# The end of the second attention on other engines: probabilities and a norm turned by DMAs, output products moved, sums of w2 in place

## The chip, the cores and the metric

One core of a Trainium2 chip runs the whole program; the others are not used. The metric is the device time of one execution in microseconds. Engines are named as the profile names them: PE (TensorE's products), PEld (its weight loads), DVE (VectorE), ACT (ScalarE), POOL (GpSimd), SP (SyncE, which issues the DMAs).

## The reference

Two transformer layers on x of shape (4, 256, 256) in float32: batches of 256 rows, width 256. Each sublayer takes a layer norm of x and adds its result to x.

```python
x = x + _L0_attn_ref(_layernorm(x), q_kernel, kv_kernel, out_kernel, q_norm_scale, k_norm_scale)
x = x + _L0_ffn_ref(_layernorm(x), w_gate, w_up, w_down)
x = x + _L1_attn_ref(_layernorm(x), W_K, W_Q, W_V, W_O)
x = x + _L1_ffn_ref(_layernorm(x), W1, W2, W3)
```

The first attention has 16 heads of 128 over 8 key and value heads, an RMS norm and a rotation on queries and keys, and a window of 128. The first feed-forward keeps two of each four hidden units. The second attention is causal with 16 heads of 128:

```python
scores = einsum('biph,biqh->biqp', k, q)
masked = scores * mask - 1e10 * (1.0 - mask)
attn = softmax(masked / sqrt(256))
z = einsum('biqp,biph->biqh', attn, v)
out = einsum('df,bqf->bqd', W_O, z_flat)
```

The second feed-forward is silu(x W1) * (x W3), a normalized Walsh-Hadamard transform over its 1024 units, and a product with W2.

## The kernel before

Everything is in float32 on chip. Rows are tiles of 128 partitions (`xs`, eight of them, two for each batch); x stays in SBUF from start to end.

Both attentions run in sixteen units. In the second, unit n is head group g = n // 4 (four heads) of batch b = n % 4. `pipelined` runs stages with lags: at step s it emits `project` of unit s, `score` of unit s - 1 and `attend` of unit s - 2, and behind them whatever `behind[s]` lists. A scheduler then orders the instructions of each engine by what it expects to be ready, within the order of emission and the hints of `issue_after`; each engine works through its own queue in order.

- `project1` makes queries, keys and values of a unit with seven block products instead of eight. `load_group1` and `right_of` prepare weights and their sums (`w_qk`, `t_qk`).
- `probabilities` (L201) takes the scores of two heads from PE, adds the mask and takes row maxima on DVE (L216), makes the bias `nb` (L221), the exponentials on ACT (L226), the reciprocal `rs` of their sums on DVE (L231), and the normalization on POOL (L234). It is called twice for each unit, for heads 0 and 1 and for heads 2 and 3.
- The products with the values need the probabilities turned. For units 0 to 13, `planes` (L253) has POOL split the float32 words of two heads into their two 16-bit halves (`pl`, L251), SP issues one DMA that transposes them (`plT`, L260), and `joined` (L263) puts the halves together again, the first head on ACT and the second on DVE (L271). For units 14 and 15, `transposed` (L239) turns them on PE (`tr_p`, L246) into PSUM and copies them out on ACT and DVE (L247).
- `attend` makes the values' products (`av`, L279 and L282) and copies them to `zT1` on ACT (L730).
- `project_out1` (L287) is the output product of one unit: sixteen records on PE (`po`, L291) and two additions into x on DVE (L297). Units 0 to 8 have theirs in steps 3 to 11, unit 12 in step 15; those of 9, 10, 11, 13, 14 and 15 stand in step 17.

`normed` (L160) makes a layer norm of one batch and turns it, either on PE (`tr_n`, L182) or, with `by_dma`, by two splits on POOL, a DMA transpose (`xplT`, L192) and two copies on ACT (L195). The second feed-forward begins with the norm of batch 0, which stands in step 16.

The second feed-forward's weights are prepared while the second attention runs. `hadamard` transforms w2: four products on PE (`ph`, L815), copied by ACT into a buffer `a`, then sums and differences on POOL in three rounds from `a` to `b`, back to `a`, and to `b` (L828); `a` and `b` are new tiles under the tags `qkw` and `qkt`. `factors_ffn1` (L839) makes the sums of w1 and w3 for one half of the hidden units, eight subtractions `t_gu` on DVE (L644), under the tag `qkw` for half 0 and `qkt` for half 1. Both halves are prepared in step 16. The tags have two buffers each, shared with the weights `w_qk` and `t_qk` of the head groups.

In the first attention, `project0` (L434) makes queries (weights `wq`) and keys and values (`wkv`) for the two row tiles of a unit. The order is queries of tile 0, keys and values of tile 0, queries of tile 1, keys and values of tile 1. Behind each product DVE makes the two parts of the rotation (`qs`, `qc`, L454), ACT the squares (L459), and for keys and values the copy of v. `rotate0` adds the parts (L473), reduces the squares (`ss`, L474), and has POOL raise the sums to a power (`r`, L493) and scale the keys (L496), which PE then turns (`tr_k`, L522).

Of the kernel before, what the change touches and what calls it, by code (L numbers as in the profile page):

```python
# [20 lines left out]
F32 = mybir.dt.float32  # L21
BF16 = mybir.dt.bfloat16
U16 = mybir.dt.uint16
AF = mybir.ActivationFunctionType
ALU = mybir.AluOpType
AX = mybir.AxisListType

P = 128
B, T, D = 4, 256, 256
NT = T // P  # L30
NC = D // P
HD = 128
NH = 16
FF = 1024
NF = FF // P
# [13 lines left out]
def two_layers(ctx, tc, consts, tables, x, wq, wkv, wo, w_gate, w_up, w_down,  # L49
               w_k, w_q, w_v, w_o, w1, w3, w2, out):  # L50
    nc = tc.nc
# [18 lines left out]
    def half(shape, name):  # L70
        return ps2.tile([P, *shape], F32, tag="half", name=name)
# [7 lines left out]
    def page(name):  # L79

        return work.tile([P, 4, T], F32, tag="page", name=name, bufs=8)
# [28 lines left out]
    tab = page("tables").rearrange("p f t -> p (f t)")[:, 0:768]  # L110
# [3 lines left out]
    wq_sb, wkv_sb = attn_weight("wq"), attn_weight("wkv")  # L114
# [29 lines left out]
    last_of = {}  # L144
# [108 lines left out]
    def planes(p, tile):  # L253


        s = tile([P, 2, 2 * 3 * P], "pl")
        words = p.rearrange("p j n -> p (j n)").bitcast(U16)
        copy_gpsimd(s, words.rearrange("p (n w) -> p w n", w=2))
        sT = tile([P, 12, P], "plT")
        nc.sync.dma_start_transpose(sT, s.rearrange("p w n -> p (w n)"))  # L260
        return sT
# [63 lines left out]
    def attention0():  # L325
        with tc.tile_pool(name="attn0", bufs=2, reuse_waits="tile", side="right") as own:
# [12 lines left out]

            def project(n, _):  # L340
                b, g = divmod(n, 4)
                held = project0(own, xnT[b], g, cos_s, sin_s)
                if g == 1 and b + 1 < B:
                    factors[b + 1] = moments(b + 1)
                if g == 2 and b + 1 < B:
                    with tc.issue_after(last_of["qc"].ins):
                        xnT[b + 1] = normed(b + 1, factors[b + 1])
                return held if n < 14 else rotated(n, held)
# [82 lines left out]
                behind, (0, 5, 4, 3, 1, 2, 6),  # L431
            )

    def project0(own, xnT, g, cos_s, sin_s):  # L434


        v = own.tile([P, NT, 2, HD], F32, tag="v", name="v", bufs=5)
        rot = []
        for t in range(NT):
            cols = slice(t * P, (t + 1) * P)  # L440
            sq = own.tile([P, 6, HD], F32, tag="sq", name="sq", bufs=2)
            qc = own.tile([P, 6, HD], F32, tag="qc", name="qc", bufs=4)
            qs = own.tile([P, 6, HD], F32, tag="qs", name="qs")

            for w, hs in ((wq_sb, slice(0, 4)), (wkv_sb, slice(4, 6))):
                pj = half([4, HD], "pj")
                n = hs.stop - hs.start
                for c in range(NC):
                    last_of[0] = nc.tensor.matmul(  # L449
                        pj, lhsT=xnT[:, c, cols], rhs=w[:, g, c, :],  # L450
                        start=(c == 0), stop=(c == NC - 1),
                    )
                for rot_to, tab in ((qs, sin_s), (qc, cos_s)):
                    last_of["qc"] = nc.vector.tensor_tensor(  # L454
                        rot_to[:, hs], pj[:, 0:n],
                        tab[:, t, hs.start // 4, :].unsqueeze(1).to_broadcast([P, n, HD]),
                        ALU.mult,
                    )
                nc.scalar.activation(sq[:, hs], pj[:, 0:n], AF.Square)  # L459
                if n == 2:  # L460
                    last_of["v", t] = nc.scalar.copy(v[:, t, :, :], pj[:, 2:4])
            rot.append((qc, qs, sq))
        return rot, v

    def rotate0(rot, by_dma, first):
# [229 lines left out]
    def attention1(finish_ffn0):  # L695
        left = left1

        def project(n, _):
            g, b = divmod(n, 4)
            if b == 1 and 1 <= g < 3:  # L700
                load_group1(g + 1)
            held = project1(left[b], gw[g])
            if g == 0 and b + 1 < B:
                with tc.issue_after(last_of["sum"].ins):
                    left[b + 1] = left_of(xn1[b + 1])
            if g == 0 and b + 2 < B:
                xn1[b + 2] = normed(b + 2, by_dma=True)
            return held

        def score(n, held):  # L710
            qk, v = held
            ps = [
                probabilities(qk[:, 0], qk[:, 1], (2 * kk, 2 * kk + 1), mask1) for kk in range(2)
            ]
            return ps if n >= B * 4 - 2 else [
                planes(p, page_of_planes) for p in ps
            ], v

        def attend(n, held):
            ps, v = held  # L720
            zT = page("zT1")
            for kk in range(2):
                pT = transposed(ps[kk]) if n >= B * 4 - 2 else joined(ps[kk], (
                    (nc.scalar.copy, slice(0, 1), last_of["copy"]),
                    (nc.vector.tensor_copy, slice(1, 2), last_of["sum"]),
                ))
                av = bank([2, T], "av1")
                for j in range(2):
                    values(v[:, 0, 2 * kk + j, :], v[:, 1, 2 * kk + j, :], pT[:, j], av[:, j, :])
                nc.scalar.copy(zT[:, 2 * kk : 2 * kk + 2, :], av)  # L730
            return zT

        def out(n, kept=False):
            g, b = divmod(n, 4)

            def emit(done):
                if not kept:
                    project_out1(bank([NT, D], "po1"), done[n], gw[g][2], b)
                else:
                    with tc.issue_after(last_of[1].ins):  # L740
                        project_out1(st([P, NT, D], "po1"), done[n], gw[g][2], b)
            return emit

        behind = {n + 3: [out(n)] for n in range(9)}
        behind[0] = [lambda _: finish_ffn0()]

        def prepare(_):
            w2h.extend(hadamard(w2_raw))
            w2h[1](_)

        behind.setdefault(11, []).append(prepare)
        for i in range(12):
            behind.setdefault(11 + i // 4, []).append(
                lambda _, i=i: w2h[2][i](last_of["planes"].ins)
            )

        def prepare_ffn1(_):
            with tc.issue_after(last_of["sum"].ins):
                r_ffn1.extend(factors_ffn1(half) for half in range(2))

        behind.setdefault(15, []).append(out(12))
        behind[16] = behind.get(16, []) + [
            lambda _: xn_f.append(normed(0)),
            prepare_ffn1,
        ]
        behind[17] = [
            out(9, True), out(13), out(10, True), out(11, True), out(14), out(15),
        ]
        pipelined((project, score, attend), (0, 1, 2), behind, (0, 1, 2))

    def st(shape, name):
# [35 lines left out]
    def hadamard(w2_raw):  # L807


        a, b = (late.tile([P, NF, D], F32, tag=t, name=f"w2_{t}") for t in ("qkw", "qkt"))  # L810

        def within(_):
            for f in range(0, NF, 2):
                ph = bank([2, D], "ph")
                nc.tensor.matmul(  # L815
                    ph, lhsT=had, rhs=w2_raw[:, f : f + 2, :], start=True, stop=True
                )
                nc.scalar.copy(a[:, f : f + 2, :], ph)

        def across(s, src, dst):  # L820
            i = src.rearrange("p (a two s) d -> p a two (s d)", two=2, s=s)
            o = dst.rearrange("p (a two s) d -> p a two (s d)", two=2, s=s)
            half = s * D // 2

            def part(k, op, cols):
                def emit(first):
                    with tc.issue_after(first):
                        nc.gpsimd.tensor_tensor(  # L828
                            o[:, :, k, cols], i[:, :, 0, cols], i[:, :, 1, cols], op
                        )  # L830
                return emit

            return [
                part(k, op, slice(n * half, (n + 1) * half))
                for k, op in enumerate((ALU.add, ALU.subtract)) for n in range(2)
            ]

        return b, within, across(1, a, b) + across(2, b, a) + across(4, a, b)

    def factors_ffn1(half):  # L840

        t = late.tile([P, 2, 4, 2, P], F32, tag=("qkw", "qkt")[half], name="t_gu")
        r = []
        for i, w in enumerate((w1_sb, w3_sb)):
            w = w[:, :, 4 * half : 4 * half + 4, :].rearrange("p c (a m) f -> p c a m f", m=2)
            r.append(right_of(*(w[:, c, :, m, :] for c in range(2) for m in range(2)),
                              [t[:, i, k] for k in range(4)]))
        return r
# [147 lines left out]
```

## Time and profile before

| what | value |
|---|---|
| median of 3 runs | 744.69 us |
| the runs | 744.12, 744.69, 949.75 us |
| the profiled execution | 745.73 us |
| its span, first to last instruction | 743.8 us |
| granted TensorE clock, mean | 1.000 |
| PE busy | 731.7 us |
| DVE, ACT, POOL busy | 464.8, 405.6, 335.1 us |
| first `sc` of unit 15 in the span | 628.80 us |
| first `gu_y` of the second feed-forward | 661.49 us |

Busy time counts when an instruction of the engine was under way. A matmul's end is modelled and its weight load overlaps it, so a busy PE may still hold short waits; the chain of work that ended last shows these as longer pieces. Most float32 products are two records. The times in the text are positions in the span of the profiled execution.

### The profile page before, as it was taken

The numbers are of one execution on the slowest core, as the hardware profiler recorded it, in microseconds if no ns is written. First come the engines' busy times: TensorE is split into PE (matmuls) and PEld (weight loads), VectorE is DVE, ScalarE is ACT, GpSimd is POOL, SyncE is SP. The second block draws the span as 40 slices with busy tenths as digits, with TensorE's granted clock in tenths as the row PEclk, the third lists the DMA queues.
The fourth block names the chain that finished last, engine by engine and source line by source line (L and its number), as shares of the span: only waits on it lengthen the run. The fifth ranks groups of instructions, "written<-read, shape, count | busy, mean of one in ns | idle before, by whom it ended". The sixth has DMA issues, their size and how long they took to land.

```text
span 743.8 us, 11642 instructions
## 1 busy us (share of the span) xinstructions
PE 731.7 (98%) x3952; PEld 598.6 (80%) x3952; DVE 464.8 (62%) x1398; ACT 405.6 (55%) x986; POOL 335.1 (45%) x481
## 2 busy tenths in 40 slices
PE   8999999999999999999999999999999999999998
PEld 5556566566666678888898999999998999899997
DVE  6999877888886516987655644464443548344433
ACT  2487887677768942222356555555555775414432
POOL 1587978887899601011125433343335674221000
PEclk9999999999999999999999999999999999999999
DMA  8733255434453442001324423442232222000100
GB/s 328 286 64 59 49 99 87 77 66 89 82 99 72 85 164 78 15 14 36 108 71 85 129 43 43 88 112 44 44 72 43 44 44 43 1 1 22 22 15 30
DMA packets 127883, 54.88 MB, mean 74 GB/s; under 512 B 121040, under 2 KB 123216, under 8 KB 127056
## 3 DMA queue, kind: packets, MB, share of 16 engines
q1 hardware_dynamic: 127824, 54.15, 31.4%
q8 instruction: 31, 0.51, 0.3%
q14 instruction: 28, 0.23, 0.1%
HBM read 22.94 MB, written 1.05 MB: 32 GB/s over the span
## 4 chain that ended last, share of the span: by engine, by line
PE 85%; DVE 8%; ACT 4%; issue 1%; DMA 1%; POOL 1%; SPq 0%; ACTq 0%; DVEq 0%; POOLq 0%
PE pj L449 10%; PE po L291 7%; PE pgu L554 7%; PE qk_x L781 7%; PE po_f L599 7%; PE po L303 7%; PE sc L214 6%; PE gu_x L856 4%; PE av L279 4%; PE qk_y L781 3%; PE v_x L787 3%; PE av L397 3%; PE sc L213 3%; PE v_zy L787 3%; PE gu_y L856 2%; PE av L282 2%
## 5 line engine op out<-in xcount | busy, mean ns | idle before, releaser
L234 POOL TENSOR_SCALAR p<-p,rs 128x128 f32<-128x128 f32 (+1 forms) x256 | 115.1, 467 | 153.3 <-DVE rs L231 150.0
L251 POOL TENSOR_SCALAR pl<-p 128x1536 uint16<-128x1536 uint16 x58 | 85.3, 1472 | 4.4 <-POOL p L234 0.5
L216 DVE CUSTOM_DVE_ANT_0 p<-sc,cst 128x128 f32<-128x128 f32 (+1 forms) x256 | 79.9, 352 | 11.1 <-PE sc L214 8.6
L271 ACT COPY pT<-plT 128x1536 uint16<-128x1536 uint16 (+1 forms) x58 | 84.0, 1511 | 0.0
L226 ACT ACTIVATE p<-p,nb,r 128x128 f32<-128x128 f32 (+1 forms) x128 | 68.3, 536 | 20.1 <-DVE nb L223 20.1
L449 PE MATMUL pj<-wq,xnT 128*128 128x512 f32 x128 | 61.2, 596 | 1.3 <-DVE qT L512 1.1
L449 PE MATMUL pj<-wkv,xnT 128*128 128x512 f32 x128 | 60.4, 593 | 0.8 <-DMA wkv<-in_wkv_dram 0.8
L226 ACT ACTIVATE p<-p,nb 128x128 f32<-128x128 f32 (+1 forms) x128 | 56.3, 448 | 5.7 <-DVE nb L221 5.7
L303 PE MATMUL po<-wo,zT 128*128 128x256 f32 x256 | 57.8, 379 | 0.0
L291 PE MATMUL po<-w_o,zT 128*128 128x256 f32 x256 | 57.7, 379 | 0.0
L156 POOL TENSOR_SCALAR ve<-mv 128x2 f32<-128x2 f32 (+1 forms) x17 | 4.3, 253 | 115.8 <-DVE mv L152 115.4
L459 ACT ACTIVATE sq<-pj 128x512 f32<-128x512 f32 x64 | 30.9, 490 | 44.0 <-DVE qc L454 43.6
L303 PEld LDWEIGHTS po<-wo,zT 128*128 128x128 f32 x256 | 48.3, 190 | 7.0 <-ACT kT L523 0.6
L291 PEld LDWEIGHTS po<-w_o,zT 128*128 128x128 f32 x256 | 47.5, 190 | 5.8
L449 PEld LDWEIGHTS pj<-wkv,xnT 128*128 128x128 f32 x128 | 24.2, 190 | 31.4 <-issue 28.2
L454 DVE TENSOR_TENSOR qs<-pj,sin_s 128x512 f32<-128x512 f32 x64 | 35.3, 552 | 12.9 <-PE pj L449 12.4
L449 PEld LDWEIGHTS pj<-wq,xnT 128*128 128x128 f32 x128 | 23.5, 190 | 24.4 <-issue 19.6
L670 ACT COPY qk<-qk_x 128x512 f32<-128x512 f32 x16 | 9.4, 586 | 57.6 <-PE qk_x L781 53.0
L279 PE MATMUL av<-pT,v 128*128 128x256 f32 x128 | 38.8, 385 | 0.9 <-ACT pT L271 0.7
L214 PE MATMUL sc<-kT,qT 128*128 128x256 f32 x128 | 38.3, 381 | 0.0
L214 PE MATMUL sc<-qk 128*128 128x256 f32 x128 | 38.2, 380 | 0.0
L251 POOL TENSOR_SCALAR qpl<-qc 128x1024 uint16<-128x1024 uint16 x20 | 28.8, 1451 | 19.1 <-PE av L401 8.3
(155 smaller groups left out, 1757.6 us busy)
## 6 DMA issues: line engine op xcount, KB each, us to landing
w<-in_w_dram SPq DMA_DIRECT2D x3, 1024.0 KB, 4.7
wq<-in_wq_dram SPq DMA_DIRECT2D x4, 512.0 KB, 7.6
wkv<-in_wkv_dram SPq DMA_DIRECT2D x4, 512.0 KB, 8.3
wo<-in_wo_dram SPq DMA_DIRECT2D x4, 512.0 KB, 10.2
w_qk<-in_w_q_dram SPq DMA_DIRECT2D x4, 512.0 KB, 4.5
w_qk<-in_w_k_dram SPq DMA_DIRECT2D x4, 512.0 KB, 5.5
w_v<-in_w_v_dram SPq DMA_DIRECT2D x4, 512.0 KB, 6.5
w_o<-in_w_o_dram SPq DMA_DIRECT2D x4, 512.0 KB, 6.5
```

Of the source, the lines that this page charges most:

```text
L214: nc.tensor.matmul(sc[:, P : 3 * P], lhsT=q[:, P:T], rhs=k, start=True, stop=True)
L216: last_of["mx"] = nc.vector.tensor_tensor_reduce(out=p[:, j, cols], in0=sc[:, cols], in1=mask[:, cols], scale=1.0, scalar=-3.0e38, op0=ALU ...
L226: last_of["exp"] = nc.scalar.activation(p[:, j, cols], p[:, j, cols], AF.Exp, bias=nb[:, j, i : i + 1], scale=SCALE1 if rq is None else rq ...
L234: nc.gpsimd.tensor_scalar(p[:, j, cols], p[:, j, cols], rs[:, j, i : i + 1], 1.0, ALU.mult, ALU.mult)
L251: last_of["planes"] = nc.gpsimd.tensor_scalar(o, i, 1.0, 1.0, ALU.mult, ALU.mult)
L271: copy(words.rearrange("p (n w) -> p w n", w=2), halves[:, :, js].rearrange("p w j n -> p w (j n)"),)
L279: nc.tensor.matmul(av, lhsT=v0, rhs=pT[:, 0:T], start=True, stop=False, skip_group_check=True)
L291: nc.tensor.matmul(po[:, t, :], lhsT=zT[:, j, t * P : (t + 1) * P], rhs=w[:, j, :], start=(t == j == 0), stop=(j == 3), skip_group_check=True,
L303: nc.tensor.matmul(po, lhsT=zTs[hd // 4][:, hd % 4, t * P : (t + 1) * P], rhs=w[:, hd, :], start=(hd == 0), stop=(hd == n - 1),)
L449: last_of[0] = nc.tensor.matmul(pj, lhsT=xnT[:, c, cols], rhs=w[:, g, c, :], start=(c == 0), stop=(c == NC - 1),)
L554: nc.tensor.matmul(o[:, j, :], lhsT=w[:, c, f0 + j, :], rhs=xnT[:, c, :], start=(c == 0), stop=(c == NC - 1),)
L781: last_of[1] = nc.tensor.matmul(o[:, j, :], lhsT=wqk[i - 1][:, j // 2, j % 2, :], rhs=x[i - 1], start=(first and j == 0), stop=True, skip_ ...
```

## The change

Five edits:

- Units 14 and 15 of the second attention go the way of the other units: `planes`, a DMA transpose and `joined`.
- The output products of units 9 and 10 are emitted ahead of the values of unit 14, those of 11 and 13 ahead of the values of unit 15. Those of 14 and 15 stay in step 17.
- The norm of batch 0 for the second feed-forward is turned by DMA.
- `hadamard` uses the tile in which w2 was loaded as its buffer `a`, and `qkw` for `b`. Both halves of `t_gu` are now under the tag `qkt`; half 0 is prepared in step 12, half 1 in step 16.
- In the first unit of the first attention the queries of both tiles come ahead of the keys and values of both.

```diff
@@ project (first attention)
-                held = project0(own, xnT[b], g, cos_s, sin_s)
+                held = project0(own, xnT[b], g, cos_s, sin_s, n == 0)
@@ project0
-        rot = []
-        for t in range(NT):
...
-            for w, hs in ((wq_sb, slice(0, 4)), (wkv_sb, slice(4, 6))):
...
-            rot.append((qc, qs, sq))
+        rot = [
+            [own.tile([P, 6, HD], F32, tag=tag, name=tag, bufs=n)
+             for tag, n in (("qc", 4), ("qs", 2), ("sq", 2))] for _ in range(NT)
+        ]
+        queries, rest = (wq_sb, slice(0, 4)), (wkv_sb, slice(4, 6))
+        parts = [(t, *part) for t in range(NT) for part in (queries, rest)]
+        if first:
+            parts = [(t, *part) for part in (queries, rest) for t in range(NT)]
+        for t, w, hs in parts:
+            qc, qs, sq = rot[t]
...
@@ score and attend (second attention)
-            return ps if n >= B * 4 - 2 else [
-                planes(p, page_of_planes) for p in ps
-            ], v
+            return [planes(p, page_of_planes) for p in ps], v
+
+        zTs, kept = {}, {14: (9, 10), 15: (11, 13)}
 
         def attend(n, held):
             ps, v = held
-            zT = page("zT1")
+            for m in kept.get(n, ()):
+                out(m, True)(zTs)
+            zTs[n] = zT = page("zT1")
             for kk in range(2):
-                pT = transposed(ps[kk]) if n >= B * 4 - 2 else joined(ps[kk], (
+                pT = joined(ps[kk], (
@@ what stands behind the steps
-        def prepare_ffn1(_):
-            with tc.issue_after(last_of["sum"].ins):
-                r_ffn1.extend(factors_ffn1(half) for half in range(2))
+        def prepare_ffn1(half):
+            def emit(_):
+                with tc.issue_after(last_of["sum"].ins):
+                    r_ffn1.append(factors_ffn1(half))
+            return emit
 
+        behind.setdefault(12, []).append(prepare_ffn1(0))
         behind.setdefault(15, []).append(out(12))
         behind[16] = behind.get(16, []) + [
-            lambda _: xn_f.append(normed(0)),
-            prepare_ffn1,
+            lambda _: xn_f.append(normed(0, by_dma=True)),
+            prepare_ffn1(1),
         ]
-        behind[17] = [
-            out(9, True), out(13), out(10, True), out(11, True), out(14), out(15),
-        ]
+        behind[17] = [out(14), out(15)]
@@ hadamard
-        a, b = (late.tile([P, NF, D], F32, tag=t, name=f"w2_{t}") for t in ("qkw", "qkt"))
+        a, b = w2_raw, late.tile([P, NF, D], F32, tag="qkw", name="w2_b")
@@ factors_ffn1
-        t = late.tile([P, 2, 4, 2, P], F32, tag=("qkw", "qkt")[half], name="t_gu")
+        t = late.tile([P, 2, 4, 2, P], F32, tag="qkt", name="t_gu")
```

## The prediction

> **What bounds the kernel now.** First the page's engine line and the shares of the chain that ended last.
>
> ```profile
> PE 731.7 (98%) x3952; PEld 598.6 (80%) x3952; DVE 464.8 (62%) x1398; ACT 405.6 (55%) x986; POOL 335.1 (45%) x481
> PE 85%; DVE 8%; ACT 4%; issue 1%; DMA 1%; POOL 1%; SPq 0%; ACTq 0%; DVEq 0%; POOLq 0%
> ```
>
> TensorE is the bound: what leaves its queue shortens the kernel, unless a wait takes its place. An average says nothing of a stage, so next the busy time by stretch (columns: stretch in us, its length, busy us and instruction counts of PE, PEld, DVE, ACT, POOL, then granted clock, DMA share, GB/s). The first row is the step before the end of the second attention, the second that end, up to the first product of the last feed-forward, the third the rest.
>
> ```profile
> 606.00:625.30 19.30, 19.30 (x132) 18.08 (x132) 11.77 (x52) 14.42 (x43) 8.43 (x13) 1.00 0.28 42
> 625.30:661.60 36.30, 36.25 (x191) 31.36 (x191) 17.93 (x68) 10.32 (x34) 11.29 (x22) 1.00 0.00 1
> 661.60:743.80 82.20, 79.01 (x581) 74.94 (x579) 35.24 (x63) 31.25 (x47) 4.05 (x6) 1.00 0.08 20
> ```
>
> In the stretch that the change rebuilds the other engines are half idle, and the DMA engines wholly. Third, the chain in order of time (start, us, what) inside that stretch.
>
> ```profile
> 625.50 3.46 PE po L291 x16
> ...
> 631.58 0.66 PE tr_p L246 x6
> 632.24 3.46 PE po L291 x16
> 635.69 0.03 issue
> 635.72 0.70 PE av L279 x2
> ...
> 636.64 0.43 PE av L279 x2
> ...
> 638.38 0.67 PE av L279 x2
> ...
> 639.93 0.44 PE tr_n L182 x4
> ...
> 645.68 15.97 PE po L291 x74
> ```
>
> Six transposes take 0.66 us, so 0.11 each. One `av` pair takes 0.43 us when its operand lies ready and 0.70 when it has to come out of PSUM first. Fourth, POOL's timeline: four normalizations and a split in the step before, then the eight normalizations of the two units in question (the last column is idle time before).
>
> ```profile
> 610.78 1.63 POOL L234 TENSOR_SCALAR p<-p,rs 128x128 f32<-128x128 f32 x4 [2.55 <-DVE rs L231]
> 612.49 1.47 POOL L251 TENSOR_SCALAR pl<-p 128x1536 uint16<-128x1536 uint16 x1
> ...
> 625.26 5.39 POOL L234 TENSOR_SCALAR p<-p,rs 128x128 f32<-128x128 f32 x8 [8.14 <-DVE rs L231]
> 633.92 1.62 POOL L234 TENSOR_SCALAR p<-p,rs 128x128 f32<-128x128 f32 x4 [3.26 <-DVE mv L152]
> ```
>
> Eight take 2 x 1.63 = 3.26 us elsewhere, 5.39 at 625.26: in that time VectorE runs eleven `t_gu` subtractions (625.08 to 629.59).
>
> **What it removes from TensorE.** Units 14 and 15 lose 24 transposes `tr_p`, the norm of batch 0 loses 4 `tr_n`: 28 x 0.11 = 3.1 us. With `tr_p` go the four `av` pairs behind it: their surplus is 2 x (0.70 - 0.43) + 2 x (0.67 - 0.43) = 1.0 us, with 0.05 of "issue" 1.05. The output products are the same seven units of 3.46 us, only in another order. Together -4.1 us. So counted, TensorE reaches the first `gu_y` at 657.4 instead of 661.5.
>
> **What it adds elsewhere.** POOL gets four splits of 1.47 and two for the norm of about 0.65 each: 7.2 us, in a stretch where it was busy 11.3 of 36.3. ACT's copies out of PSUM (0.48 each) become joins of 1.0, and the norm's copy of 0.59 two of 0.67: 2.8 us more, beside 10.3. VectorE's four copies go from 0.55 to 0.60. SP's queue gets four transposes and one, each needing 3.7 and 3.1 us from issue to landing, ahead of the norm's transpose for batch 2 and the stores, which are not due before 670. All this is hidden, if the probabilities land before TensorE needs them; the cover is now the moved products. I follow that by rows.
>
> TensorE: scores of unit 15 with one product in between until 631.9, `out(9)` and `out(10)` until 638.3, values of unit 14 until 640.9, `out(11)` and `out(13)` until 647.9, values of unit 15 until 650.5, whose second pair of heads is due at 649.2.
>
> Unit 14: POOL starts at 625.26 as before. Half of the subtractions are now made three steps earlier and three of the rest still run until 626.2; of the surplus of 2.1 us I keep 0.75 (the first two of the eight took 0.71 and 0.89 against 0.37 and 0.48). First pair: 625.3 + 1.6 + 0.75 + 1.5 = 629.2, landed 632.9. Second: 629.2 + 1.6 + 1.5 = 632.4 with hand-overs, landed 636.1, joined on VectorE 636.7. Here is the wait that the change puts in: on VectorE this join stands ahead of the bias (`nb`) of unit 15's second pair, the two statistics and the reciprocal that unit 15's normalizations need. Bias 636.9, four exponentials on ACT of 0.39 and 0.49 (1.8) until 638.7, ACT's part of the join until 639.7: TensorE wants it at 639.6, a wait of 0.1.
>
> Unit 15: statistics 0.7 and reciprocal on VectorE until 637.7, POOL normalizes to 639.4, the norm's epsilon 0.2, split to 641.1, second pair to 642.8, the power `rstd` 0.7, split to 645.0, landed 648.7, joined on ACT 649.7. Wanted at 649.2 plus 0.1, so TensorE waits 0.4. Both waits together: +0.5 us, the ends 0 (each hand-over 0.1 shorter) and 1.3 (POOL's whole surplus of 2.1 instead of 0.75 would add 1.35, less what overlaps).
>
> The norm by DMA: its splits follow on POOL until 646.3, landed 649.5, copied by ACT behind the join at 651.1, the four `xs` of left_of at 652.3. First use is `gu_y` at 657.9, so 5.6 us of products cover it; without them every microsecond would show.
>
> A rule speaks on the rest of that collision. Row first: 5.39 us against 3.26 with subtractions beside them. The Trainium skill, "SBUF — State Buffer", section "Who interferes with whom", says that a VectorE instruction with two SBUF inputs and a GpSimd instruction that reads SBUF exclude each other for a whole instruction. By that rule the three remaining subtractions of 0.42 would cost POOL 1.26 instead of my 0.75, and the wait would be 1.0 instead of 0.5; the direction of the trace agrees.
>
> **Sums of w2 in place, and the earlier half of `t_gu`.** The same instructions on other buffers: 0. The eight subtractions of half 0 now run beside unit 11's normalizations near 582. At the same rate POOL and the transposes behind it are 0.75 late there; that unit's joins ended on ACT at 594.24 for a use at 595.16, and ACT comes to the second join only when the first is done. Cover 0.9; without it the cost is 0.75. I take 0.
>
> **First unit's queries first.** Two lines of the timeline.
>
> ```profile
> 9.35 1.98 PE L449 MATMUL pj<-wkv,xnT 128*128 128x512 f32 x4 [0.82 <-DMA wkv<-in_wkv_dram]
> ...
> 23.04 0.44 PE L522 MATMUL tr_k<-cst,qc 128*128 128x128 f32 x2 [0.31 <-POOL qc L496]
> ```
>
> TensorE has up to 1.1 us of hole before `wkv` lands, and the second queries would fill it. But at 23.04 it waits for POOL, whose power needs both reductions of VectorE, and VectorE works without a gap from 9.69 (the landing of x2 and x3) to 18.1 through the same list of operations in another order. The gain can be all of 1.1; the loss, if a later `wkv` product keeps VectorE waiting, one product of 1.7. The rows lie near nothing: -0.1.
>
> **Sum.** -4.1 + 0.5 - 0.1 = -3.7. The profiled execution took 745.73 for a span of 743.8, so 742.0 for a span of 740.1. It lies 1.04 above the median of 744.69; against that the same change gives 741.0.
>
> **Rivals.** Chance of the forecast (waits of 0 to 1.3, 740.2 to 741.8): 0.68.
>
> *The first unit gives its whole hole* (0.06): 1.1 instead of 0.1, 740.0. For it the 0.82 of idle; against it the busy VectorE.
>
> *The last values are late* (0.17). The two flights in series decide. Transposes of `plT` landed in 3.6 to 5.3 us, median 3.7. One slow flight adds 1.6, full contention on POOL 1.35: 742.4 to 744.0. For it: VectorE's order puts unit 14's join ahead of unit 15's bias. Against: nothing else moves on the DMA engines in that stretch (share 0.00).
>
> *Slower* (0.05): the same series with both flights at 5.3 (3.2), POOL contended in unit 14 (1.35) and in unit 15 (2.1): 6.65 more wait, 741.0 + 6.65 = 747.7. The place is the `av` of unit 15's second pair; it decides from 3.7 us of further lateness on, where the gain is used up. Against: no subtraction is left beside unit 15.
>
> *The transposes lie open* (0.02): if the order of products gave no cover, four flights of 3.7 and four splits of 1.47 would stand on the path, 20.7 - 4.2 = +16.5, 761.2. Against: rows show 13.8 us of products in front of the values. The Trainium skill, "VectorE: DVE Perf Modes", section "Rules for kernel authors", advises TensorE for a 128x128 transpose where PSUM will do as the destination, which speaks for this case; no row here shows an open flight of that kind.
>
> *No gain* (0.02): TensorE reaches `gu_y` early and waits for the norm by DMA or for `t_gu`: 744.7. It needs 3.7 us more than the 5.6 of cover.
>
> **Numbers.** Likeliest 741.0. The range 739.8 to 743.6 holds the forecast, the first rival and most of the second, and leaves out less than 2 in 10. A measurement of this kernel can tell about 2% (14.9 us) from no change: faster by more 0.01, within 0.96, slower by more 0.03.
>
> **What would show it.** In the changed profile: no `tr_p` at all in the second attention; first `gu_y` near 658 of the span; the `av` pairs at 0.43 but for waits under 1 us ahead of unit 15's second pair, named with ACT `pT`; unit 14's normalizations near 4 us for eight; the span up to 560 shifted by less than 0.5. A wait over 2 us at those `av`, a wait of `gu_y` for `xs`, or a shift above 1 us at 560 would make it wrong.

## The result and the profile after

| | kernel before | changed kernel |
|---|---|---|
| median | 744.45 us | 742.09 us (8 runs, 741.09 to 743.62) |
| ratio to before | | 0.9969, 95% interval 0.9959 to 0.9978 |
| profiled execution, span | 745.73, 743.8 us | 743.62, 741.8 us |
| first `po` of unit 12 | 625.34 | 625.59 |
| first `gu_y` | 661.49 | 659.54 |
| the stretch between these two | 36.15 | 33.95 |

The change brings 2.4 us, 0.3%: clear of 1 by its interval, far inside the 2% that the prediction counted as a change. 3.7 were forecast (741.0 us, range 739.8 to 743.6). One execution of the kernel before (949.75 us) and one of a later experiment (1087.03 us at a granted clock of 0.656) were slow and are left out of the ratios. The starts are those of PE's timeline. The last row is the measure used below, from one profiled execution of each run: it leaves out what happens before 625 us, which differs by a few tenths between executions (the changed kernel's profiled one is 0.25 us behind there), and behind `gu_y` the kernels are alike. The profile of the changed kernel, engine line and shares of the chain that ended last:

```profile
PE 728.4 (98%) x3924; PEld 596.2 (80%) x3924; DVE 467.3 (63%) x1398; ACT 409.3 (55%) x987; POOL 341.1 (46%) x487
PE 74%; DVE 8%; POOL 7%; issue 4%; ACT 4%; DMA 2%; SPq 0%; POOLq 0%; ACTq 0%; DVEq 0%
```

28 matmul records are gone, the 24 `tr_p` and 4 `tr_n`. PE's part of the chain fell from 85% to 74%: the chain now leaves PE. The stretches show where:

```profile
606.00:625.30 19.30, 19.30 (x133) 18.10 (x132) 11.95 (x53) 14.16 (x41) 8.82 (x12) 1.00 0.23 44
625.30:659.70 34.40, 33.02 (x166) 29.10 (x165) 16.86 (x61) 13.75 (x36) 16.74 (x28) 1.00 0.35 54
```

Before, PE was busy for 36.25 of 36.30 us here. Now it is idle for 1.4, and the DMA share is 0.35 instead of 0.00. PE's timeline names the place (the last column is idle time and what ended it):

```profile
641.12 0.70 PE L279 MATMUL av<-pT,v 128*128 128x256 f32 x2 [1.07 <-ACT pT L271]
...
651.22 0.70 PE L279 MATMUL av<-pT,v 128*128 128x256 f32 x2 [0.31 <-ACT pT L271]
```

These are the second pairs of heads of units 14 and 15. Each of them also takes 0.70 in the chain instead of 0.43, so the two cost 1.07 + 0.31 + 2 x 0.27 = 1.9 us. The chain of waits tells what was late:

```profile
630.91 1.48 POOL pl L251
632.39 0.02 issue
632.41 5.10 DMA plT<-pl
637.50 0.02 issue
637.53 0.60 DVE pT L271
638.13 0.04 DVE nb L221
638.17 0.66 DVE st L151 x2
638.83 0.08 DVE rs L231
...
641.00 1.47 POOL pl L251
642.47 1.62 POOL p L234 x4
644.09 0.68 POOL rstd L157
...
646.24 3.84 DMA plT<-pl
650.09 0.02 issue
650.11 1.06 ACT pT L271
```

The flight of unit 14's second pair took 5.10 us. Behind it, in VectorE's queue, stand unit 15's bias and reciprocals, and so POOL's work, the second flight and ACT's join. It is the series that the prediction followed, 1.4 us later from its first flight on.

### The profile page after: what moved, and what is told of

Read it like the earlier page. It is cut to its first block, busy times and chain, and to the rows that moved or that the text cites. A ratio compares the mean times of both kernels' runs of the same rounds, so it can differ in the third digit from the quotient of the medians.

```text
span 741.8 us, 11618 instructions
## 1 busy us (share of the span) xinstructions
PE 728.4 (98%) x3924; PEld 596.2 (80%) x3924; DVE 467.3 (63%) x1398; ACT 409.3 (55%) x987; POOL 341.1 (46%) x487
## 4 chain that ended last, share of the span: by engine, by line
PE 74%; DVE 8%; POOL 7%; issue 4%; ACT 4%; DMA 2%; SPq 0%; POOLq 0%; ACTq 0%; DVEq 0%
PE pj L452 10%; PE pgu L556 7%; PE po_f L601 7%; PE po L303 7%; PE qk_x L786 5%; PE po L291 5%; PE sc L214 5%; PE gu_x L861 4%; PE av L397 3%; PE qk_y L786 3%; PE v_x L792 3%; PE sc L213 3%; PE av L279 2%; POOL p L234 2%; PE gu_y L861 2%
## 5 line engine op out<-in xcount | busy, mean ns | idle before, releaser
L271 ACT COPY pT<-plT 128x768 uint16<-128x768 uint16 (+1 forms) x62 | 88.2, 1479 | 9.6 <-DMA plT<-pl 9.6
L251 POOL TENSOR_SCALAR pl<-p 128x1536 uint16<-128x1536 uint16 x62 | 91.3, 1473 | 4.6 <-POOL p L234 0.5
L462 ACT ACTIVATE sq<-pj 128x512 f32<-128x512 f32 (+1 forms) x64 | 31.0, 491 | 42.2 <-DVE qc L457 41.8
L457 DVE TENSOR_TENSOR qs<-pj,sin_s 128x512 f32<-128x512 f32 (+1 forms) x64 | 35.3, 552 | 13.4 <-PE pj L452 12.9
```

Of the source, the lines that this page charges most:

```text
L251: last_of["planes"] = nc.gpsimd.tensor_scalar(o, i, 1.0, 1.0, ALU.mult, ALU.mult)
L271: copy(words.rearrange("p (n w) -> p w n", w=2), halves[:, :, js].rearrange("p w j n -> p w (j n)"),)
```

## The experiments

Theory: the loss against the forecast is that first flight, passed on through VectorE's queue. Rivals: POOL, slowed by the subtractions of `t_gu`; the first unit's new order; and, for the long flight itself, chance.

**The joins stand later.**

```diff
@@ attend, the two joins of unit 14
-                    (nc.scalar.copy, slice(0, 1), last_of["copy"]),
-                    (nc.vector.tensor_copy, slice(1, 2), last_of["sum"]),
+                    (nc.scalar.copy, slice(0, 1),
+                     ex_of[15, kk] if n == 14 else last_of["copy"]),
+                    (nc.vector.tensor_copy, slice(1, 2),
+                     rs_of[15, kk] if n == 14 else last_of["sum"]),
```

`ex_of` and `rs_of` hold the last exponential and the reciprocal of unit 15's pairs.

> Edit: of the changed kernel, only the place in the queues of unit 14's two joins is moved: VectorE's behind the reciprocals of unit 15, ACT's behind unit 15's exponentials. Theory (a series of two flights): in the changed kernel the flight of unit 14's second pair (632.41 to 637.50, 5.10 us) holds VectorE's join, behind which the bias of unit 15's second pair stands, and so unit 15's statistics, normalizations, splits and its own flight; with the joins later that row of work starts when its scores are there, near 635, the waits of TensorE (1.23 at unit 14's second pair, about 0.1 and 0.47 at unit 15) shrink to under 0.3 together unless the flight itself is late, and the time is 1 to 2 us under that of the changed kernel, 740 to 741. Rival (POOL, contended by the subtractions of t_gu, is what is late): unit 15's probabilities come as late as before, TensorE still waits about 1.8 us there, and the time stays within 0.5 us of the changed kernel.

Measured: 741.04 us where the kernel before took 745.66 on the same chip, ratio 0.9939 (0.9926 to 0.9951); the changed kernel's was 0.9969. VectorE's timeline:

```profile
632.73 0.13 DVE L221 TENSOR_SCALAR nb<-mx 128x4 f32<-128x4 f32 x1
...
634.65 0.58 DVE L271 COPY pT<-plT 128x768 uint16<-128x768 uint16 x1
...
635.77 0.17 DVE L231 RECIPROCAL rs<-sm 128x4 f32<-128x4 f32 x1
636.64 0.61 DVE L271 COPY pT<-plT 128x768 uint16<-128x768 uint16 x1 [0.70 <-DMA plT<-pl]
```

The bias now comes at 632.73 instead of 638.02, and both reciprocals stand ahead of the join of 636.64. The flight was long again, 4.85 us, but nothing of unit 15 hangs on it. PE shows no wait in the stretch:

```profile
625.30:657.20 31.90, 31.90 (x162) 28.45 (x161) 15.13 (x59) 13.25 (x34) 17.28 (x28) 1.00 0.36 58
```

The stretch is 32.04 us: 1.91 shorter than in the changed kernel, 4.11 shorter than before. POOL's contention was left in (unit 14's eight normalizations take 3.74 us), so it wasn't what was late. In this kernel the norm's statistics and its power on POOL, at 629.95 and 633.17, also stand ahead of unit 15's normalizations; what that alone is worth is not separated.

**The transposes back on TensorE.**

```diff
-            return [planes(p, page_of_planes) for p in ps], v
+            return ps if n >= B * 4 - 2 else [planes(p, page_of_planes) for p in ps], v
...
-                pT = joined(ps[kk], (
+                pT = transposed(ps[kk]) if n >= B * 4 - 2 else joined(ps[kk], (
...
-            lambda _: xn_f.append(normed(0, by_dma=True)),
+            lambda _: xn_f.append(normed(0)),
```

> Edit: the changed kernel, but units 14 and 15 and the norm of batch 0 are turned on TensorE again, as in the kernel before; the moved products, the sums of w2 in place, the earlier half of t_gu and the first unit's order stay. Theory (what the prediction counted): the 28 transposes and the surplus of the av pairs, 4.1 us, come back on TensorE and the waits of 1.8 us at the av go, so it is about 2.3 us slower than the changed kernel, and equal to the kernel before within 0.5 us: the moved products alone give nothing. Rival (the moved products give part of the gain by filling holes of the kernel before, such as the 0.05 of issue and the waits of the transposes): 0.5 to 1.5 us faster than the kernel before, and the transposes are worth that much less.

Measured: 745.72 beside 745.66, ratio 1.0000 (0.9991 to 1.0009), a span of 743.8 as before. The moved products, w2 in place, the earlier half of `t_gu` and the first unit's order, with the transposes undone, bring nothing together that the interval would show. Of the rival's 0.5 to 1.5 us it leaves only the lowest end.

**The first unit's order undone, on top of the later joins.**

```diff
-                held = project0(own, xnT[b], g, cos_s, sin_s, n == 0)
+                held = project0(own, xnT[b], g, cos_s, sin_s, False)
```

> Edit: as the kernel with the joins later, but the first unit's products stand in the order of the kernel before (queries, then keys and values, block by block). Theory (the first unit's new order is a small loss: the trace of the changed kernel lies 0.08 us behind that of before at 26 us, and 0.25 behind from 290 to 620): 0.1 to 0.3 us faster than with the joins later alone. Rival (the shift of 0.25 is a spread between executions, and the order is worth nothing or the hole of up to 1.1 us): the same within 0.1 us, or slower by up to 1.

Measured: 740.96 beside 741.04 with the new order, 0.9939 both; the spans are 739.1 and 739.3. The 0.1 us is no more than what medians of five runs leave open, so no effect of the order is shown. The 0.25 us of the changed kernel's trace is a spread between executions: the kernel with the later joins has the new order too, and its first `po` comes at 624.97, 0.37 ahead of the kernel before.

**Eight idle products fewer.**

```diff
-    for i in range(10):
+    for i in range(2):
```

> Edit: the changed kernel with 2 instead of 10 idle products at its start, which reference and outputs don't need; every later instruction of TensorE keeps its place, but counts 8 products (16 records of PE and PEld) less from the start of its queue. Theory (a flight of plT is long when a packet of the instruction queue falls into it: of the flights of 4.4 to 5.3 us in the second attention of both traces all hold a 16 KB packet of that queue, and such packets come once in about 256 instructions of TensorE): the packets come 8 to 16 instructions of TensorE later, 1.5 to 3.5 us in the second attention, so that other flights are long: the packet of 634.4 comes near 636 to 638, behind unit 14's second flight, which then takes 3.6 to 3.8 us, and the wait of 1.2 us at that av is gone or under 0.3; the long flights near 400, 438 and 497 change likewise, since their packets come after their landing. Rival (long flights are a matter of chance or of the transposes themselves): the same flights are long as in the changed kernel, or long ones are found without a packet in them. The time itself: no difference above 1.5 us.

The queue of instructions (q8 in the profile) moves 31 packets of 16 KB in an execution. Flights of `plT` from issue to landing, in us, and the start of the packet nearest behind the issue:

| issued at (changed kernel) | flight, packet | with 2 idle products: flight, packet |
|---|---|---|
| 399.52 | 5.35, 402.81 | 3.64, 405.55 |
| 438.01 | 5.32, 441.31 | 3.65, 443.63 |
| 459.14 | 4.82, 460.30 | 3.65, 463.68 |
| 477.12 | 4.83, 479.19 | 3.65, 483.69 |
| 496.75 | 5.30, 500.07 | 3.65, 502.91 |
| 632.41 | 5.10, 634.36 | 3.65, 638.05 |

All six long flights of the second attention have become normal, and two others are long (4.84 issued at 441.72, 4.90 at 614.79), with packets at 443.63 and 616.78 in them. The DMA view from 632.0 to 638.5, first of the changed kernel, then of this one (tenths busy in 40 slices of 0.16 us):

```profile
DMA  9910000001999990000000000999999000000000
...
q8 instruction: 1, 0.02, 0.9%
```

```profile
DMA  9999930000000699999999998000000000000300
...
q8 instruction: 1, 0.02, 0.9%
```

A normal flight moves its packets in one go, 634.1 to 636.1 in the second row (the 3 behind it is the instruction packet). In the first the same flight all but stands still from 634.4 to 636.1, in which time one instruction packet of 0.92 us moves, and then goes on. The rival of chance falls. At PE's wait of 641.12 in the changed kernel there is none here:

```profile
641.10 0.60 PE L279 MATMUL av<-pT,v 128*128 128x256 f32 x2
```

A wait of PEld of 0.3 at unit 15 is left, and the stretch is 32.44 us with the joins where the change put them, 0.40 above the one without waits. (The median was 742.81, ratio 0.9966, no clear gain over the changed kernel: with two idle products TensorE stands idle for 3.12 us ahead of the first norm's transposes, the eight records on `wq` behind them take 5.49 us instead of 3.70, and at 24 us this execution is 0.78 us behind the changed kernel. Why those records are slower is not shown.)

**The cover taken away.**

```diff
-        zTs, kept = {}, {14: (9, 10), 15: (11, 13)}
+        zTs, kept = {}, {}
...
-        behind[17] = [out(14), out(15)]
+        behind[17] = [
+            out(9, True), out(13), out(10, True), out(11, True), out(14), out(15),
+        ]
```

> Edit: the changed kernel, but the output products of units 9, 10, 11 and 13 stand behind the values of unit 15 again, as in the kernel before (with one of them between the values of unit 14, where the queue of TensorE had it before). All transposes of units 14, 15 and of the norm still run as DMAs, so this is the DMA part of the change without its cover. Theory (a series that overlaps with POOL and with what products are left between): the values of unit 14 wait for flights that land near 633 and 636 to 637.5, those of unit 15 for flights near 643 to 644 and 648 to 650, and behind the last stand five units of products of 3.46 us and half of a pair; the first gu_y comes at 664 to 665.5 of the span instead of 659.7, so 4 to 6 us slower than the changed kernel and 2 to 4 slower than the kernel before: near 747 to 749. Rival (the prediction's, that all four flights and splits lie open one behind the other): 16.5 us slower than before, 761. Second rival (the cover isn't needed): the time of the changed kernel.

Measured: 748.42 beside 745.59, ratio 1.0038 (1.0024 to 1.0052), `gu_y` at 664.14, as the theory had it. So the DMA part alone makes the kernel slower, the moved products alone do nothing, and both together gain. The waits:

```profile
PE av L279 <- ACT pT L271: 4.8, 3, 2.0
```

The stretch is 7.36 us longer than with the later joins; 4.8 are waits, 0.8 the surplus of the three pairs that waited, and another part is the granted clock (third column from the right):

```profile
640.20:644.90 4.70, 2.75 (x14) 2.09 (x12) 2.48 (x3) 1.63 (x2) 4.46 (x8) 1.00 0.45 84
644.90:646.00 1.10, 1.04 (x5) 0.99 (x6) 0.34 (x1) 0.01 (x1) 0.80 (x1) 0.81 0.93 176
646.00:647.30 1.30, 1.30 (x6) 1.12 (x5) 0.00 (x0) 0.00 (x0) 0.00 (x0) 0.50 1.11 207
647.30:649.00 1.70, 1.70 (x6) 0.98 (x4) 0.61 (x1) 1.26 (x2) 0.00 (x0) 0.50 0.61 113
649.00:651.00 2.00, 2.00 (x13) 1.82 (x13) 1.33 (x5) 1.88 (x4) 0.00 (x0) 1.00 0.00 0
```

After a wait of 2.01 us PE runs at half its clock until 649. At 0.81 and 0.50 these busy times hold some 1.7 us more than at full clock: 1.04 x 0.19 + 1.30 x 0.5 + 1.70 x 0.5.

**The norm of batch 0 on TensorE.**

```diff
-            lambda _: xn_f.append(normed(0, by_dma=True)),
+            lambda _: xn_f.append(normed(0)),
```

> Edit: the changed kernel, but the norm of batch 0 for the last feed-forward is turned by four transposes tr_n on TensorE, as in the kernel before; units 14 and 15 stay with DMAs. Theory (place in the queue): tr_n stands behind the values of unit 14, ahead of the two moved products of 6.91 us, and waits for POOL, whose rstd ends at 644.05 in the changed kernel; TensorE reaches it at 642.4 to 642.7 and waits for about 2 us, besides 0.44 for four transposes; the waits of unit 15 (0.6) go in return, and the time is 1.5 to 2.5 us above that of the changed kernel. Rival (the prediction's account, 4 transposes of 0.11 and nothing else): 0.44 above the changed kernel.

Measured: 748.02 to 749.70 us, ratio 1.0047 (1.0030 to 1.0063), some 6 us above the changed kernel: outside both expectations. A second profile of the same kernel:

> The kernel of the run before last once more, the norm of batch 0 turned by four tr_n on TensorE and nothing else of the changed kernel undone: it took some 6 us more than the changed kernel, where 1.5 to 2.5 were expected and the prediction's account gave 0.44. Theory (queue): TensorE stands still at tr_n behind the values of unit 14, and what it waits for is xn on VectorE, which follows rstd on POOL (644.7 at the earliest), and in VectorE's queue may stand behind a join of unit 15 as well: then the wait at tr_n is 3 to 6 us in this profile, named with DVE xn, and the rest of the stretch has none. Rival (the rest is a wait that tr_n causes elsewhere, such as a PSUM buffer that is free later or the join of unit 15 behind the copy of tr_n on ACT): the wait at tr_n stays under 3 us, and waits of 2 us or more stand at the values of unit 15 or at po.

Measured: 748.28, a stretch of 39.76 us, 5.81 above the changed kernel. Its waits, PE's timeline, and the clock:

```profile
PE tr_n L182 <- DVE xn L171: 3.7, 1, 3.7
PE av L279 <- ACT pT L271: 0.5, 1, 0.5
```

```profile
644.36 1.11 PE L182 MATMUL tr_n<-cst,xn 128*128 128x128 f32 x4 [3.72 <-DVE xn L171]
645.26 9.21 PE L291 MATMUL po<-w_o,zT 128*128 128x256 f32 x32
```

```profile
645.50:648.00 2.50, 2.50 (x7) 1.93 (x7) 0.30 (x2) 1.21 (x4) 0.00 (x0) 0.50 0.80 149
648.00:649.00 1.00, 1.00 (x4) 0.81 (x3) 1.00 (x4) 0.97 (x1) 0.00 (x0) 0.50 0.00 0
649.00:650.00 1.00, 1.00 (x5) 0.76 (x5) 0.45 (x2) 0.00 (x0) 0.00 (x0) 0.71 0.00 0
```

The wait is that of the theory: `tr_n` stands behind the values of unit 14 and ahead of 6.91 us of products, and TensorE comes to it before POOL has `rstd`. The second half of the loss was in neither: after 3.72 us of idling, `tr_n` takes 1.11 us instead of the 0.60 of the timeline before, and the two units of products 9.21 instead of the 7.07 that the changed kernel's timeline has for them, 2.6 us more in all, at a granted clock of 0.50. The wait, the `tr_n` and the surplus of the products, 3.72 + 1.11 + 2.14, are 6.97. Of the changed kernel's 1.91 only one wait of 0.54 with its pair's 0.27 is left, 1.1 less: 5.87 where 5.81 were measured.

**Contention beside POOL.** The earlier half of `t_gu` put back:

```diff
-        behind.setdefault(12, []).append(prepare_ffn1(0))
...
+            prepare_ffn1(0),
             prepare_ffn1(1),
```

> Edit: the changed kernel, but the earlier half of t_gu is prepared in the step where the kernel before prepared both, so that eleven of the sixteen subtractions again run beside the normalizations of unit 14; its buffer stays. Theory (contention, counted as the prediction did): POOL's eight normalizations of unit 14 take about 5.4 us, as in the kernel before, instead of 3.76; the second pair is issued 1.6 us later, near 634, and lands at 637.7, or at 639.3 when it is held up; the waits at the values of units 14 and 15 grow by 0.5 to 2 us together, and the time by as much. Rival (VectorE's queue decides, which the eight subtractions lengthen by 3.4 us, or nothing does): more than 2 us, or within 0.3 of the changed kernel.

Measured: 744.00 us, ratio 0.9978 (0.9968 to 0.9987), a stretch of 34.41, 0.46 above the changed kernel's, though its flight was held up less, 4.19 us. The next run, with the changed kernel's instructions on the same chip, took 742.42 to 742.96, this one 743.12 to 744.32: a loss of some 1.3 us. POOL's normalizations:

```profile
624.55 2.96 POOL L234 TENSOR_SCALAR p<-p,rs 128x128 f32<-128x128 f32 x4 [8.16 <-DVE rs L231]
...
629.09 2.20 POOL L234 TENSOR_SCALAR p<-p,rs 128x128 f32<-128x128 f32 x4
```

They take 5.16 us instead of 3.76, about what was expected. But the waits at the values did not grow, they are 0.7 us in all; a new one stands earlier, at a score of unit 15, behind VectorE's queue, where two of the subtractions took 2.21 us together (0.42 each elsewhere) while POOL's split ran. The score starts 1.04 us late and takes 0.11 longer; that is all of the 1.16 by which this stretch is longer than the next run's 33.25, whose waits at the values are 0.7 us too. So the loss stands where the rival had it, in VectorE's queue, though smaller than it said. POOL's lateness is real (the second pair is issued 8.25 us behind the first `po` of unit 12 instead of 6.82), but TensorE, held up at the score, comes to the values later as well.

```profile
627.17 2.21 DVE L646 TENSOR_TENSOR t_gu<-w,t_gu 128x256 f32<-128x256 f32 x2
```

```profile
PE sc L213 <- DVE x L297: 0.9, 1, 0.9
PE av L279 <- ACT pT L271: 0.7, 2, 0.5
```

The later half put back a step:

```diff
-            prepare_ffn1(1),
...
-        behind[17] = [out(14), out(15)]
+        behind[17] = [out(14), out(15), prepare_ffn1(1)]
```

> Edit: the changed kernel, but the later half of t_gu is prepared one step later, so that no subtraction runs beside the normalizations of unit 14. Theory (contention is the surplus of 3.76 over 3.26): the eight normalizations take 3.3 us, the second pair of unit 14 is issued 0.5 us earlier, near 631.9, and TensorE's waits at the values shrink from 1.8 to about 1.3 if that flight is held up again, else to 0.1. The time falls by 0.5 to 1.7. By the rule of the Trainium skill's SBUF page that a VectorE instruction with two SBUF inputs and a GpSimd one exclude each other, 1.26 would be to be had on POOL. Rival (what is late is the flight alone): the issue moves by less than 0.2 us.

The edit reached no queue: `last_of["sum"]`, on which the hint rests, isn't renewed between the two steps, and every engine's instructions stand as in the changed kernel. What was expected of contention stays untested; the run is a second execution of the changed kernel, 742.72 us, ratio 0.9963 (0.9948 to 0.9977). In that it tells something: the same instructions had a flight of 4.53 us instead of 5.10, and a stretch of 33.25 instead of 33.95.

```profile
631.87 4.53 DMA plT<-pl
```

## Why the prediction was right or wrong

The median of 742.09 lies in the stated range of 739.8 to 743.6, but above the 740.2 to 741.8 that had the chance of 0.68. The mechanism was right, and one term of the sum was too small.

- *TensorE loses 4.1 us* (28 transposes of 0.11, the surplus of four `av` pairs). Right: 36.15 to 32.04 with the later joins, 4.11, where no wait is left; and all of it comes back with the transposes.
- *Two waits, +0.5 us, ends 0 and 1.3.* The mechanism, both places and the queue behind the join were right; the term was mis-sized, 1.91 in the profiled execution (33.95 - 32.04) and 1.21 in the second one. Its wrong part is the flight, taken as 3.7 and landed 636.1: it took 5.10 and 4.53. With a flight of 3.65 (two idle products) the same term is 0.40. A smaller part is the surplus of a pair that waits, 0.27: the prediction took it off for all four pairs and put it down to an operand out of PSUM, but the two that wait for `pT` in the changed kernel take 0.70 as well, 0.54 together. All this is the rival "last values late", which got 0.17. The median is just under its 742.4 to 744.0; the profiled execution's 743.62 has to be held against 743.4 to 745.0, since the prediction put that execution 1.04 above the median, and lies in it. The reason against that rival, that nothing else moves in that stretch by a DMA share of 0.00, was the wrong view: the mean share doesn't show one packet of 16 KB. The packet of 633.23 was in the trace of before, inside the flight that the prediction placed at 632.4 to 636.1, as the DMA view of before from 632.0 to 638.5 shows:

```profile
DMA  0000000400000000000010000000000000000000
...
q8 instruction: 1, 0.02, 1.1%
```

- *Contention on POOL, +0.75.* 0.50: the first four of unit 14 take 2.13 us with three subtractions beside them and 1.63 without. The 1.26 by the rule of the Trainium skill, "SBUF — State Buffer", "Who interferes with whom", is not reached; its direction is seen on both engines (two subtractions took 2.21 beside POOL's split).
- *The norm by DMA, worth four transposes, 0.44.* As a sum right, as the worth of this edit beside the others wrong: with the products moved, TensorE is at `tr_n` 3.7 us before its operand, and without the DMA the change would have been a loss. The cover was counted rightly: `xs` is ready at 653.5, `gu_y` starts at 659.54 and doesn't wait.
- *w2 in place and half 0 of `t_gu`, 0.* Right: unit 11's first four normalizations went from 1.62 to 2.13 us, and TensorE's distance to the kernel before stays at 0.25 from 290 to 629.
- *First unit, -0.1.* Nothing is shown, 0.1 either way. The hole was filled, TensorE no longer waits for `wkv`, but the wait for POOL at a `tr_k` grew from 0.31 to 0.89, in line with the reason against the first rival, the busy VectorE.
- *The transposes lie open, 761.2.* Without the cover it is 748.42. The sum put four flights and splits behind each other, but POOL, two units of products and the flights overlap; the rival's mechanism is real and its price was six times too high (2.8 instead of 16.5).
- *What would show it.* No `tr_p`, 3.76 us for unit 14's eight normalizations, a shift of 0.25 at 560 and 0.31 us ahead of unit 15's second pair came as told; the 1.07 at unit 14's second pair, where 0.1 was expected, and `gu_y` at 659.5 instead of 658 did not.

## What to carry to other kernels

Take work off the engine that bounds a kernel only together with what fills its place; each half alone was worth nothing or a loss. When a wait for a transfer enters an engine's queue, look at what stands behind it there: moving the copies of one unit behind the instructions that others wait for nearly doubled the gain (ratio 0.9969 to 0.9939). And price a transfer by its slow flights when a packet of another queue is due in it; a mean share of the DMA engines doesn't show that.

## What the runs showed of the hardware

- A DMA transpose all but stands still around a packet of the instruction queue. Behind 385 us ten profiles (all but the one of 1087.03 us) have 312 flights of `plT`. The 256 with no such packet 0.9 to 3.4 us behind their issue take 3.6 to 3.9 us. With one 0.9 to 2.6 us behind it, all 30 take 4.2 to 5.2; with one 3.1 to 3.4 behind it, 26 take 3.7 to 5.5, and what decides among these is not shown. The packets move with TensorE's instructions: 32 records fewer at the start put the packet of 634.36 3.1 us later against its neighbours, at some 9.6 records a microsecond (331 in 34.4 us) the time of 30. The Trainium skill, "Runtime: NRT & Kernel Launch", "Instruction fetch mechanics", has blocks of 16 KiB for 256 instructions that an engine's sequencer fetches by a DMA queue of its own, mostly hidden; the 31 packets for 7848 records of PE and PEld, 253 each, agree. Hidden it is for TensorE itself (busy for 31.90 of 31.90 us with the later joins, with a packet at 632.88), but not for a transpose beside it. Why all sixteen engines pause is not shown.
- A wait of TensorE can cost more than its length. After waits of 1.07 and, without the cover, 1.73 us the granted clock stays at 1.00. After 2.01 us it is 0.50 from 645.59 to 649.00, which cost another 1.7 us; in the wait of 3.72 us it falls to 0.50 at 642.75 and stays there until 649.57, another 2.6 us. The two stretches are 3.41 us and twice that, so where a wait lies against such steps may count beside its length; no run tests it. The Trainium skill, "TensorE: Matmul & The Clock Gate", "Part 1: The HAM clock gate", gives half the clock after an idle window of some 3.4 us; the 0.50 agrees, but the gap of 2.01 was shorter, and the 2.75 us ahead of it were busy throughout.
